# Two attention layers on one core: a fourth split step, outputs accumulated in DRAM, and projections in half blocks

## The chip, the cores and the metric

The kernel runs on one core of one Trainium2 chip. The core has a matrix engine (TensorE, PE in the profile, with its weight loads as PEld), a vector engine (VectorE, DVE), an activation engine (ScalarE, ACT), a general engine (GpSimd, POOL) and a queue engine (SyncE, SP) that here only issues transfers. Each engine executes its own instructions in order and waits for the others by semaphores. The metric is the device time of one execution in microseconds, the median of several runs.

## The reference, cut to what matters

The input x has 4 images of 64 x 64 tokens with 256 channels, so N = 4096 tokens each. Two attention layers follow one another, with no division by the root of the width:

```python
# layer 0: q, k are 32 wide, v is 256 wide
q, k, v = x @ Wq + bq, x @ Wk + bk, x @ Wv + bv
x = gamma * softmax(q @ k.T) @ v + x
# layer 1: f, g are 32 wide, v is 128 wide
f, g, v = x @ Wf + bf, x @ Wg + bg, x @ Wh + bh
x = x + (softmax(g @ f.T) @ v) @ Wo + bo
```

All values are float32. Layer 1 of an image needs layer 0 of the same image for all of its tokens, since every token is a key; different images are independent.

## The kernel before, in words

The work of an image is two stages, layer 0 and layer 1, and the images follow one another: one list of steps (b, l, j, i) is made at the end of `fast_path`, with b the image, l the layer, j the query block and i the step over keys. Layer 0 has 16 query blocks of 256 tokens with 8 steps of 512 keys. Layer 1 has 8 query blocks of 512 tokens with 16 steps of 256 keys.

A step's `scores` (L505) are products of keys and queries into one PSUM tile `st`, which has a single buffer; ScalarE takes the exponential of it (L517) into p. No maximum is subtracted. Scores are issued two steps ahead of the products that use them.

The products of p with the values need float32 accuracy, and there are two ways to get it. A *whole* step multiplies p and v as float32; each such product stands as two matmul instructions in the trace. A *split* step uses the faster fp32r type for parts. ScalarE makes a second exponential, with a slightly lowered exponent, rounded to fp32r: `high` (L515). VectorE subtracts it from p to get `low` (L522) and combines the two into `d` (L527). Three products (high with the values' part h, low with l, d with d) into two accumulators give the result (L536 in layer 0, L557 in layer 1). In layer 0 all steps are split. In layer 1 the steps 2, 7 and 12 of each block's 16 are, and the others are whole. In layer 1 VectorE also adds up p over the steps into `p_sum` (L698; at the first step a copy, L696), from which the softmax's denominators come; in layer 0 a column of ones in the values gives them.

Between the steps' own instructions lie *units*. `project_units` makes three or four for a block of 512 tokens: `transpose_unit` (squares of 32 x 32, which transfers have put in place, are transposed on VectorE, L381, and x is cut into two fp32r parts, L387 and L388), `qk_unit` (four products of 512 columns, L412; evictions L422 to L425; the result goes to DRAM, L428, and comes back as keys and queries by transfers from POOL, L472), and `v_unit` (products L442, evictions). The transposed x, the parts for two channel halves and the loaded squares lie in tiles `xT` (one buffer) and `squares` (five buffers of one channel half). `end_first` normalizes a layer-0 block and adds the residual (L585): the new x goes to DRAM for layer 1's projections (`x1_dram`, L590), and the same plus the output bias, added on POOL (L593), goes to a second DRAM tensor (`x1_res`, L594). `end_second` multiplies a layer-1 block by Wo (L624), gets denominators (L625 and L627), and adds the loaded `x1_res` rows to the scaled output on VectorE (L628); SP then writes `out` (L630). `load_old` (L605) loads those rows four steps ahead of a block's end.

The units of a block are spread evenly over its steps: `pace` and `upto` hand out so many at each step. Layer 1's projection of block (j-3)/2 is done in layer 0's block j for odd j from 3 on. Block 7 can't be done there, because its tokens come from the end of layer 0: it is done in layer 1's first block, whose last two steps (14 and 15) need its keys and values. The next image's layer-0 projections are done one block per query block of layer 1. Image 0's own first three blocks are projected before its first step, the other five in its first five steps.

The order of the instructions on an engine is laid down when the program is built. It follows the order of the text as a priority, but lets through what is expected to be ready sooner, so the trace can show another order than the text.

Of the kernel before, what the change touches and what calls it, by code (L numbers as in the profile page):

```python
# [60 lines left out]
S = 32  # L61
DOWN = 2.0**-13
EPS = 2.0**-12
AHEAD = 3

# [168 lines left out]
def fast_path(ctx: ExitStack, tc: tile.TileContext, x, w0, w1, wo, bo, gamma, out, off):  # L234
# [13 lines left out]
    split = [[l == 0 or i % 5 == 2 for i in range(NI[l])] for l in range(2)]  # L248
# [18 lines left out]
    def load_squares(key, tokens):  # L267

        turned[key] = []
        for c in range(NCC):  # L270
            t = work.tile([P, QB], F32, tag="squares", bufs=5, name=f"squares_{key[0]}_{key[1]}_{key[2]}_{c}")
            for a in range(P // S):
                ch = c * P + a * S
                nc.sync.dma_start(
                    t[a * S : (a + 1) * S, :].rearrange("j (b i) -> j b i", i=S),
                    tokens[:, ch : ch + S].rearrange("(b j) i -> j b i", j=S),
                )
            turned[key].append(t)

    def load_block(b, j):  # L280
        if b < B and j < NB:
            load_squares((b, 0, j), x[b, j * QB : (j + 1) * QB, :])


    x_nat = {}

    def load_first(j):
        if j < NB:
            x_nat[j] = []
            for n in range(j * NT, (j + 1) * NT):  # L290
                x_nat[j].append(data.tile([P, C], F32, tag="v1", bufs=V1, name=f"x_nat_{n}"))
                nc.sync.dma_start(x_nat[j][-1], x[0, n * P : (n + 1) * P, :])

    load_first(0)
    load_first(1)
# [8 lines left out]
    seen_v = const.tile([P, 2, B * NB, 2], F32, name="seen_v")  # L304
# [61 lines left out]
    xT, x_parts, k_t, v_t = {}, {}, {}, {}  # L366
    qk_dram, x1_dram, x1_res = {}, {}, {}
    q_t = {}


    def transpose_unit(b, l, j):
        def issue():
            xT[b, l, j] = data.tile([P, NCC, QB], F32, tag="xT", name=f"xT_{b}_{l}_{j}")
            for c in range(NCC):
                if b == l == 0:
                    ps = side_psum(f"psx_{j}_{c}")
                    for t in range(NT):
                        nc.tensor.transpose(ps[:, t * P : (t + 1) * P], x_nat[j][t][:, c * P : (c + 1) * P], ident)
                    nc.scalar.copy(xT[b, l, j][:, c, :], ps)
                else:  # L380
                    nc.vector.transpose(xT[b, l, j][:, c, :], turned[b, l, j][c])  # L381
            x_parts[b, l, j] = []
            for c in range(NCC):
                parts = [
                    work.tile([P, QB], F32R, tag="squares", bufs=5, name=f"x{what}_{b}_{l}_{j}_{c}") for what in "hl"
                ]
                nc.scalar.copy(parts[0], xT[b, l, j][:, c, :])  # L387
                nc.vector.tensor_sub(parts[1], xT[b, l, j][:, c, :], parts[0].bitcast(F32))  # L388
                x_parts[b, l, j].append(parts)
            if b == l == 0:  # L390
                load_first(j + 2)
            elif l == 0:
                load_block(b, j + 1)
            elif j == NB - 1:
                load_block(b + 1, 0)
# [3 lines left out]
    def split_values(v, h, low, d, seen):  # L399
        nc.scalar.activation(h, v, AF.Copy, scale=1.0 - DOWN)  # L400
        nc.scalar.activation(low, v, AF.Abs, accum_out=seen)
        nc.vector.scalar_tensor_tensor(d, h.bitcast(F32), -1.0 - EPS, v, ALU.mult, ALU.add)
        nc.vector.scalar_tensor_tensor(low, d.bitcast(F32), 1.0 / EPS, h.bitcast(F32), ALU.mult, ALU.add)
# [393 lines left out]
```

## Time and profile before

| | us |
|---|---|
| median of 3 runs | 3222.8 (3222.76 to 3225.62) |
| the profiled execution | 3222.18 |
| its span, first to last instruction | 3220.4 |
| PE busy | 3166.5 (98%) |
| DVE busy | 2691.5 (84%) |
| ACT busy | 1988.8 (62%) |
| POOL busy | 661.3 (21%) |

A row of the groups names the line, the engine, the operation, output and inputs with their shapes, the count, then the busy time, the mean duration in ns, and after a bar the time that the engine was idle just before them and what ended it. A row of the windows has a stretch in us from the span's start, its length, the busy time of PE, PEld, DVE, ACT and POOL with instruction counts, the granted share of the TensorE clock, and the transfers' share and rate. A line in order of time has start, duration, engine, line, operation, tiles and count, and in brackets the idle time before it with what ended it. SPq is the issuing of a transfer on SP.

### The profile page before, as it was taken

Reading aid. Unit: us, or ns where it says so; the run is one execution under the profiler, and the core shown is the slowest. Engines: PE = TensorE matmul, PEld = TensorE weight load, DVE = VectorE, ACT = ScalarE, POOL = GpSimd, SP = SyncE. Lnnn points to the kernel's source line nnn. Section 1 sums busy time; section 2 is a strip of 40 time slices with the busy share of each in tenths; the row PEclk is TensorE's granted clock in tenths of the full one; section 3 lists DMA queues with packets and bytes.
Section 4 is the critical chain, followed back from the end, with each engine's and each line's share of the span. In section 5 each row is a group of like instructions: output and inputs, shape, how many; then the busy total and the mean of one; then the engine's idle time right before and its main releaser. Section 6 shows DMA issues by size and latency. Waiting matters only on the chain. (4 is left out here: it accounts for less than half of the span.)

```text
span 3220.4 us, 51144 instructions
## 1 busy us (share of the span) xinstructions
PE 3166.5 (98%) x19460; PEld 2613.0 (81%) x19460; DVE 2691.5 (84%) x3181; ACT 1988.8 (62%) x2483; POOL 661.3 (21%) x784
## 2 busy tenths in 40 slices
PE   8999999999999999999999999999999999999998
PEld 7999997566799999655679999966558999995554
DVE  7888888888888888788888888878888888887776
ACT  6666666655566666565556666655555666665554
POOL 3222223000232222200022222310002222241000
PEclk9999999999999999999999999999999999999999
DMA  4111123221212112322121112232222211121110
GB/s 120 47 47 44 50 50 83 56 53 49 59 44 54 44 52 49 79 53 53 49 64 42 49 50 50 61 70 52 51 52 57 53 41 47 46 70 47 36 36 31
DMA packets 368653, 172.16 MB, mean 53 GB/s; under 512 B 257392, under 2 KB 343664, under 8 KB 368400
## 3 DMA queue, kind: packets, MB, share of 16 engines
q1 hardware_dynamic: 342528, 134.29, 16.0%
q0 software_dynamic: 24960, 34.18, 4.5%
q8 instruction: 157, 2.57, 0.3%
q14 instruction: 96, 0.79, 0.1%
q10 hardware_dynamic: 912, 0.33, 0.0%
HBM read 99.22 MB, written 67.11 MB: 52 GB/s over the span
## 5 line engine op out<-in xcount | busy, mean ns | idle before, releaser
L517 ACT ACTIVATE p<-st 128x1024 f32<-128x1024 f32 x1024 | 1044.5, 1020 | 393.6 <-PE st L505 369.5
L515 ACT ACTIVATE high<-st,down 128x1024 fp32r<-128x1024 f32 x608 | 678.8, 1116 | 683.6 <-PE st L505 572.7
L527 DVE SCALAR_TENSOR_TENSOR d<-low,high 128x1024 fp32r<-128x1024 f32 x608 | 761.2, 1252 | 208.3 <-PE acc L536 202.9
L522 DVE TENSOR_TENSOR low<-p,high 128x1024 fp32r<-128x1024 f32 x608 | 810.6, 1333 | 134.2 <-ACT p L517 134.2
L557 PE MATMUL acc<-p,v 128*128 128x512 f32 x1664 | 795.2, 597 | 0.0
L505 PE MATMUL st<-q,k 128*128 128x256 f32 (+1 forms) x3072 | 778.6, 361 | 8.4 <-ACT p L517 8.3
L698 DVE TENSOR_TENSOR p_sum<-p_sum,p 128x1024 f32<-128x1024 f32 x480 | 587.1, 1223 | 60.7 <-ACT p L517 47.5
L505 PEld LDWEIGHTS st<-q,k 128*128 128x128 f32 x3072 | 461.2, 189 | 210.7 <-ACT p L517 113.3
L536 PE MATMUL acc<-v0d,d 128*128 128x258 f32 x4096 | 591.7, 284 | 1.7 <-DVE d L527 1.6
L536 PE MATMUL acc<-v0h,high 128*128 128x258 f32 x4096 | 588.6, 283 | 1.6 <-ACT high L515 1.6
L536 PE MATMUL acc<-v0l,low 128*128 128x258 f32 x4096 | 587.0, 283 | 0.5 <-DVE low L522 0.5
L536 PEld LDWEIGHTS acc<-v0d,d 128*128 128x128 f32 x4096 | 533.1, 189 | 6.7 <-DVE d L527 3.6
L536 PEld LDWEIGHTS acc<-v0h,high 128*128 128x128 f32 x4096 | 534.1, 190 | 3.4 <-ACT high L515 2.0
L536 PEld LDWEIGHTS acc<-v0l,low 128*128 128x128 f32 x4096 | 532.7, 189 | 0.8 <-DVE low L522 0.7
L557 PEld LDWEIGHTS acc<-p,v 128*128 128x128 f32 x1664 | 308.4, 190 | 214.3 <-issue 184.7
L593 POOL TENSOR_TENSOR x_res<-x,bo 128x256 f32<-128x256 f32 x128 | 216.3, 1690 | 889.9 <-DVE g L583 482.0
L472 POOL DMA_DIRECT2D q<-qk_dram x252 | 123.9, 501 | 1166.1 <-PE st L505 1143.0
L676 POOL TENSOR_TENSOR x_res<-x_res,bv 128x256 f32<-128x256 f32 x128 | 189.6, 1482 | 114.4 <-DMA x_res<-in_x 85.0
L442 PE MATMUL psv<-wv,xT 128*128 128x128 f32 (+1 forms) x1024 | 194.8, 331 | 6.8 <-DVE qk L423 6.1
L442 PEld LDWEIGHTS psv<-wv,xT 128*128 128x128 f32 x1024 | 159.6, 192 | 29.8 <-DVE qk L423 8.5
L472 POOL DMA_DIRECT2D k<-qk_dram x224 | 109.6, 500 | 245.2 <-PE st L505 140.3
L388 DVE TENSOR_TENSOR xl<-xT,xh 128x512 fp32r<-128x512 f32 x128 | 87.1, 683 | 5.1 <-ACT xh L387 4.7
(96 smaller groups left out, 1701.9 us busy)
## 6 DMA issues: line engine op xcount, KB each, us to landing
x_res<-in_x SPq DMA_DIRECT2D x128, 128.0 KB, 2.2
qk_dram<-qk_parts SPq DMA_DIRECT2D x64, 256.0 KB, 2.1
x_dram<-x SPq DMA_DIRECT2D x128, 128.0 KB, 1.7
x_res<-x_res SPq DMA_DIRECT2D x128, 128.0 KB, 1.7
squares<-x_dram SPq DMA_DIRECT2D x256, 64.0 KB, 2.3
x_old<-x_res SPq DMA_DIRECT2D x128, 128.0 KB, 2.0
out<-x_old SPq DMA_DIRECT2D x128, 128.0 KB, 1.7
q<-qk_dram POOLq DMA_DIRECT2D x252, 64.0 KB, 2.1
```

What stands on the lines that cost most here:

```text
L442: nc.tensor.matmul(ps[:, t, :], xT[key][:, c, (t0 + t) * P : (t0 + t + 1) * P], wv[l][:, c, :], start=(c == 0), stop=(c == NCC - 1),)
L472: nc.gpsimd.dma_start(dst[n * D : (n + 1) * D, :], parts[h, which])
L505: nc.tensor.matmul(st[:, g, :], k_t[b, l, kt // NT][:, kt % NT * P : (kt % NT + 1) * P], q_t[b, l, j * n // QB][:, q0 : q0 + n], start=Tru ...
L515: nc.scalar.activation(self.high, s_flat, AF.Exp, bias=down)
L517: nc.scalar.activation(self.p, s_flat, AF.Exp)
L522: nc.vector.tensor_sub(self.low, self.p, self.high.bitcast(F32))
L527: nc.vector.scalar_tensor_tensor(self.d, self.low.bitcast(F32), -1.0 / EPS, self.high.bitcast(F32), ALU.mult, ALU.add)
L536: nc.tensor.matmul(acc[2 * s + which][:, :W], p[:, g * QB0 + s * P : g * QB0 + (s + 1) * P], v0[self.i][v][:, g, :], start=self.first and ...
L557: nc.tensor.matmul(acc[which], v[:, g, :], p[:, g * QB : (g + 1) * QB], start=first and g == 0, stop=last and g == G[1] - 1,)
L593: nc.gpsimd.tensor_add(x_old[s], x_new[s], bo_sb)
L676: nc.gpsimd.tensor_add(x_res[b, j][t], x_res[b, j][t], bv)
L698: nc.vector.tensor_add(p_sum, p_sum, s.p)
```

## The change

In layer 1, four steps per block (`SPLIT1` = 2, 6, 10, 14) are split instead of three. Layer 0's residual with the bias goes to `out` directly; `x1_res` and `load_old` are gone. Layer 1's output is scaled on ScalarE and added to `out` in DRAM by an accumulating transfer from POOL. The sum of p begins with an addition at step 1. Projections are made for half blocks of 256 tokens, with the two channel halves in one instruction where that is possible; a unit's products have 256 columns. The loads of squares are issued half by half: behind the projection of the half before. At the start of image 0 two halves are under way, the odd ones in buffers of the split values. The even spreading is replaced by `plan`, which puts each unit at a step: in layer 0's block j the three units of half j-2 at steps 0, 4 and 5; in layer 1's first block halves 14 and 15 at steps 0, 2, 3 and 6, 8, 9; the next image's halves every seven steps from step 12 of the first block on; a finished block's end units at steps 1 and following of the next.

The diff, cut to its core; what stands at the places left out is the same renaming of blocks to halves, buffers and loads of image 0's start:

```diff
+SPLIT1 = (2, 6, 10, 14)
...
-    split = [[l == 0 or i % 5 == 2 for i in range(NI[l])] for l in range(2)]
+    NH = N // QB0
+    split = [[l == 0 or i in SPLIT1 for i in range(NI[l])] for l in range(2)]
...
     def load_squares(key, tokens):
-        turned[key] = []
+        t = work.tile([P, NCC, QB0], F32, tag="squares", bufs=2, name="squares_" + "_".join(map(str, key)))
         for c in range(NCC):
-            t = work.tile([P, QB], F32, tag="squares", bufs=5, name=f"squares_{key[0]}_{key[1]}_{key[2]}_{c}")
             for a in range(P // S):
                 ch = c * P + a * S
                 nc.sync.dma_start(
-                    t[a * S : (a + 1) * S, :].rearrange("j (b i) -> j b i", i=S),
+                    t[a * S : (a + 1) * S, c, :].rearrange("j (b i) -> j b i", i=S),
                     tokens[:, ch : ch + S].rearrange("(b j) i -> j b i", j=S),
                 )
-            turned[key].append(t)
+        turned[key] = t
...
+            lead = b == l == 0 and h % 2 == 1
+            tag = "v1_parts" if lead else "xT"
+            xT[key] = data.tile([P, NCC, QB0], F32, tag=tag, bufs=LEAD_BUFS if lead else 1, name=f"xT_{b}_{l}_{h}")
...
+                nc.vector.transpose(
+                    xT[key].rearrange("p c n -> p (c n)"), turned[key].rearrange("p c n -> p (c n)")
+                )
...
+            nc.scalar.copy(x_parts[key][0], xT[key])
+            nc.vector.tensor_sub(x_parts[key][1], xT[key], x_parts[key][0].bitcast(F32))
...
-            nc.sync.dma_start(qk_dram[key].rearrange("h w d n -> (h w d) n"), parts.bitcast(F32))
+            nc.sync.dma_start(qk_dram[b, l, j].rearrange("h w d n -> (h w d) n")[:, cols], parts.bitcast(F32))
+            halves[b, l, j] = part + 1
+            if l == 0 and b > 0:
+                load_half(b, h + 1)
+            elif l == 1 and h == NH - 1:
+                load_half(b + 1, 0)
+            elif l == 1:
+                load_squares((b, 1, h + 1), waiting.pop((b, h + 1)))
...
+        def add_up(self, p_sum):
+            if self.l == 0:
+                return
+            if self.i == 0:
+                first_p.append(self.p)
+            elif self.i == 1:
+                nc.vector.tensor_add(p_sum, first_p.pop(0), self.p)
+            else:
+                nc.vector.tensor_add(p_sum, p_sum, self.p)
...
-                if part == QB // QB0 - 1 and s == NS - 1:
-                    load_squares((b, 1, jj), x1_dram[b, jj])
+                if s == NS - 1:
+                    tokens = x1_dram[b, jj][part * QB0 : (part + 1) * QB0, :]
+                    if j == 0:
+                        load_squares((b, 1, j), tokens)
+                    else:
+                        waiting[b, j] = tokens
                 nc.gpsimd.tensor_add(x_old[s], x_new[s], bo_sb)
-                nc.sync.dma_start(x1_res[b, jj][row : row + P, :], x_old[s])
+                nc.sync.dma_start(out[b, n * P - b * N : (n + 1) * P - b * N, :], x_old[s])
...
-                nc.vector.scalar_tensor_tensor(y[t], ps[:, :C], inverse[:, 1, n : n + 1], y[t], ALU.mult, ALU.add)
+                y = small(f"y_{key}_{t}")
+                nc.scalar.activation(y, ps[:, :C], AF.Copy, scale=inverse[:, 1, n : n + 1])
                 row = j * QB + t * P
-                nc.sync.dma_start(out[b, row : row + P, :], y[t])
+                nc.gpsimd.dma_start(out[b, row : row + P, :], y, accum_op=ALU.add)
...
+    def plan(b, l, j, ends):
+        units = {}
+        def put(i, *some):
+            units.setdefault(i, []).extend(some)
+        if l == 0:
+            if j >= 2:
+                t, qk, v = project_units(b, 1, j - 2)
+                put(0, t), put(4, qk), put(5, v)
+            for n, u in enumerate(ends):
+                put(1 + n, u)
+            return units
+        if j == 0:
+            for n, u in enumerate(ends):
+                put(1 + n, u)
+            for n, h in enumerate((NH - 2, NH - 1)):
+                t, qk, v = project_units(b, 1, h)
+                put(6 * n, t), put(6 * n + 2, qk), put(6 * n + 3, v)
+        else:
+            for n, u in enumerate(ends):
+                put(1 + n, u)
+        if b + 1 < B:
+            for h in range(NH):
+                i = 12 + 7 * h - j * NI[1]
+                for n, u in zip((0, 2, 3), project_units(b + 1, 0, h)):
+                    if 0 <= i + n < NI[1]:
+                        put(i + n, u)
+        return units
...
-        if l == 1 and s.i == NI[1] - 4:
-            load_old(b, j)
...
-        pace = NI[l] - (5 if l == 1 else 1)
-        upto = min(len(units), -(-len(units) * (s.i + 1) // pace))
-        todo = units[done:upto]
-        done = upto
+        s.add_up(p_sum)
+        todo = units.get(s.i, [])
```

## The prediction

> **What bounds the kernel now.** I read the page's first section, the groups of instructions, a table of windows by stage, and the order of time of single engines around the one place where the windows differ.
>
> ```profile
> PE 3166.5 (98%) x19460; PEld 2613.0 (81%) x19460; DVE 2691.5 (84%) x3181; ACT 1988.8 (62%) x2483; POOL 661.3 (21%) x784
> ...
> L628 DVE SCALAR_TENSOR_TENSOR x_old<-pso,inverse,x_old 128x256 f32<-128x256 f32 x128 | 61.5, 481 | 3.4 <-DVE inverse L627 0.3 <-DMA x_old<-x_res 0.3
> L696 DVE COPY p_sum<-p 128x1024 f32<-128x1024 f32 x32 | 23.8, 745 | 2.7 <-ACT p L517 0.2
> ...
> core 0: us, PE busy (x) PEld busy (x) DVE busy (x) ACT busy (x) POOL busy (x), PEclk, DMA share, GB/s
> 854.90:1306.80 451.90, 451.90 (x3718) 448.31 (x3717) 385.97 (x435) 293.59 (x356) 130.23 (x126) 1.00 0.20 51
> 1311.80:1363.90 52.10, 46.43 (x149) 26.37 (x147) 41.42 (x51) 28.95 (x43) 6.28 (x10) 0.97 0.33 71
> 1445.90:1487.70 41.80, 41.56 (x141) 25.01 (x139) 35.51 (x44) 24.62 (x31) 1.96 (x4) 1.00 0.20 51
> 2902.60:2947.00 44.40, 40.12 (x128) 21.84 (x126) 33.76 (x39) 23.61 (x32) 7.41 (x10) 1.00 0.22 56
> 3020.00:3057.20 37.20, 36.89 (x121) 21.27 (x119) 29.30 (x34) 19.94 (x21) 1.96 (x4) 1.00 0.12 36
> ```
>
> The rows are the first layer of image 1, the first and a later query block of its second layer, then the same two of image 3. TensorE is the bound almost everywhere, but its busy time hides small stalls, because matmul records overlap. I therefore use distances between starts. A row of twelve whole products takes 5.31 us including the last one's tail: 0.43 us each. Two 512-column products of parts span 0.62 us where one lasts 0.39: 0.23 us apart. Those of 258 columns are 0.12 apart, those of 256 too. So a plain second-layer step is 4 x 0.43 + 2 x 0.23 = 2.18 us of TensorE, a split one 8 x 0.233 = 1.86. Priced so, all matmuls sum to about 3125 us. The first layer (451.9 us) lies on this floor. A later second-layer block is 0.8 us above it with projections in it (41.8 against 41.0) and 0.6 without. The *first* block of each second layer is 8.1, 9.7, 9.7 and 6.4 us above it: 33.9 us together. The first query block of all lies 9.3 us above (57.1 against 47.8), and 8 us at the end hold no compute.
>
> Why the first block stalls, in image 1 (start, duration, engine):
>
> ```profile
> 1319.36 4.11 SPq L274 DMA_DIRECT2D squares<-x_dram  x8
> 1327.57 0.70 DVE L381 STREAM_TRANSPOSE xT<-squares 128x512 f32<-128x512 f32 x1
> 1333.62 0.70 DVE L381 STREAM_TRANSPOSE xT<-squares 128x512 f32<-128x512 f32 x1
> 1340.45 0.34 SPq L428 DMA_DIRECT2D qk_dram<-qk_parts  x1
> 1342.98 1.98 POOL L472 DMA_DIRECT2D k<-qk_dram  x4 [24.53 <-DMA qk_dram<-qk_parts]
> 1353.44 1.99 PE L442 MATMUL psv<-wv,xT 128*128 128x256 f32 x8 [1.84 <-DVE qk L423]
> 1355.08 0.81 PE L505 MATMUL st<-q,k 128*128 128x512 f32 x2
> ```
>
> Block 7's tokens exist only when the first layer has ended. From there one chain runs: squares, two transposes, projection, DRAM, keys. The scores of step 14 need those keys; they land near 1346.6 (last issue 1344.5 plus 2.1), and scores that would be due near 1340 start at 1355.1. The squares were in by 1325.3, but VectorE's second transpose stood behind other work until 1333.6; and the next image's projections stood ahead of the scores in TensorE's order and waited for VectorE themselves. In image 3, without them, the scores start as the keys land (2938.7).
>
> **What the Trainium skill says.** "TensorE: Matmul & The Clock Gate", part 1, says that an idle array falls to half clock for a window of about 3.4 us. The trace agrees: the granted clock is 0.50 from 1345.0 to 1348.4 and again from 2140.3 to 2143.7, both in these first blocks, so such a stall costs about 1.7 us more. "DMA: Bandwidth & Descriptors", SWDGE vs HWDGE vs iDMA, says that accumulating transfers come from GpSimd alone; its rules for kernel authors add that an accumulate must wait for the earlier write of the same bytes. No run here shows an accumulate yet. Here the earlier write lies a layer back. "ScalarE: Activation LUTs", What happens when an `exp` ACTIVATE runs, gives about 0.09 us for each pointer operand; the trace agrees (1116 ns with a bias tile, 1020 without).
>
> **The change part by part.** The sum is made on the profiled execution (span 3220.4, its own time 3222.2); the median 3222.8 is 0.6 higher, which I ignore.
>
> 1. *A fourth split step in each of 32 second-layer blocks.* Four whole products at 0.43 (1.72 us) become six at 0.233 (1.40): 0.32 less. 32 x 0.32 = **-10 us**. ScalarE gets 32 exponentials of 1.12 (36 us), VectorE 32 x 2.44 (78 us), where its low and d take 1.22 each in this layer.
>
> 2. *First block of the second layer.* Half 14 is now done at steps 0 to 3. Half 15's residual moves from step 0 to 2, yet in the trace it was already written only at 1316.7, where step 2 starts. Its squares queue on SP behind the x1 and out writes and half 14's qk write, so I put them at 1320.5, plus 4.1 of issues and 2.3 of landing: 1327. The transpose is one instruction now, planned at step 6 (1326), qk at step 8 (1330), four steps later than before. In image 3 the way from the end of that projection to the scores took 10.1 us (2928.6 to 2938.7); with half-width evictions I take 9. So keys land near 1340.5, scores of 14 are due at 1339.8, and no other projection stands in the way before step 14, as the next image begins at step 12. Step 14 is split now and wants low and d soon after. I take 3 us left in each image: 12 instead of 33.9, **-22 us**. Bounds: nothing left (-34), or all of it left (0).
>
> 3. *Later blocks.* A split step's chain from its scores: exponentials 0.2+2.0, low 1.2, d 1.2, and up to one addition of p_sum between (1.1): 4.6 to 5.7 us. TensorE has 5.3 us of work meanwhile, so it waits up to 0.4 us, unless an output or a projection falls into those two steps. Today this shows once in an image-3 block (0.45 us at step 12). Of the new steps 2 and 6 are covered by outputs at steps 1 to 4; 10 and 14 often aren't. 28 later blocks x 0.2 = **+5 us**. Bounds: -8 (VectorE is relieved) to +15.
>
> 4. *Outputs.* Removed: 128 VectorE operations of 481 ns, 128 loads and 128 residual writes; the residual write now goes to out, so SP issues 256 fewer. Added: 128 ScalarE scalings and 128 accumulates on POOL. A scaling is bounded by 0.39 (the 128x258 copy out of PSUM) and 0.48 (plus the skill's pointer); I take 0.48, 61 us. An accumulate's issue is bounded by 0.50 (32 rows) and 0.86 (128 rows of wqk_whole); I take 0.86, 110 us on an engine 21% busy. Queued behind a waiting accumulate on POOL are the next block's q and, in the last block, the next image's keys; POOL now waits 35 to 40 us for scores before each q, so that hides it; uncovered it would cost the scores directly. Hidden in the middle. At the end the last accumulate lands 1.7 (a plain write) to 3.7 us (a read first) after issue: **+1 us** (0 to 3).
>
> 5. *Sum of p.* 32 copies of 745 ns go, and the addition starts at step 1; VectorE -24 us, hidden. The first p is held a step longer; the third step's p is in another tag, so a buffer is there.
>
> 6. *Half blocks.* TensorE: a block's four 512-column projections (4 x 0.233) become eight of 256 (8 x 0.118): 64 x 0.012 = **+1 us**. VectorE's qk pair (740 and 694 ns) has some 0.37 us of fixed part beyond 512 elements at 0.96 per ns, paid twice: +24 us; ScalarE likewise +23. SP: 448 loads of squares become 896 of half size, at 0.51 us of issue: +229 us, and 64 more qk writes; POOL 32 more short key issues in the first image. SP's queue has no other user that is short of time, because a half's squares are asked for five steps (12 us) before their transpose and need 6.4. With two buffers a load waits until the previous half's projection has read its parts; it is issued just behind that projection, so this wait is short. If that cover is gone, the transpose is late and everything behind it on VectorE.
>
> 7. *Start.* The first block of image 0 lies 9.3 us above the floor, with ScalarE and VectorE nearly full. Two halves in flight in separate buffers overlap more, the extra fixed parts take some back: **-3 us** (-7 to +4).
>
> Engine totals after: VectorE -61-24+78+24+3 (values of the new split) = +20 on 2691; ScalarE 36+61+23 = +120 on 1989. Neither becomes the bound on average.
>
> Sum: -10 -22 +5 +1 +1 -3 = -28: 3222.8 - 28 = **3195 us**.
>
> **The rivals.**
>
> *The wait stays.* Half 15 is projected at step 8 instead of 4, and the order on an engine isn't that of the text: the second transpose came 8 us after its data. If that recurs, 8.5 us stay per image: 3195 + 4 x 5.5 = 3217. For it: the chain is as long as the four steps left. Against it: one transpose instead of two, no second projection in the way.
>
> *More goes than I count.* The first blocks lose all (-12), the start 3 more and the later blocks 8: 3172. For it: more distance at every transpose. Against it: the uncovered splits.
>
> *Late d, slower.* There are 128 split steps. VectorE runs in order, and if one more addition of p_sum (1.13 us between starts) stands ahead of each d, TensorE waits that much: 128 x 1.13 = +145, 3340. It decides from 28/128 = 0.22 us per split step on. For it: four steps need 4 x 1.13 + 2 x 1.13 = 6.8 us of VectorE in 8.4, before projections; and scores have one buffer, which a split step holds 2.8 us (scores 0.46, exponentials 2.0, gaps 0.3) against a step of 1.86, and a plain one 1.83 against 2.18, so that three plain steps only just win it back. Against it: VectorE is 15% free over a block (35.5 of 41.8 now); 2.7 us are taken off per block (part 4 and 5) for 2.4 added.
>
> **How the numbers follow.** The likeliest (3181 to 3210) has 0.60, more goes 0.17, the wait stays 0.13, late d 0.10. Changes within 0.2% (6.4 us) can hardly be told from none. Faster: 0.60 + 0.17 + half of the second rival (3217 lies at the border 3216.4) = 0.83; same 0.07; slower 0.10. Range: from 3172 (middle of "more goes") to 3214; outside lie half of that, most of "the wait stays" and "late d", about 2 in 10.
>
> **What would show it.** Right: 52.1 and 44.4 us for the first blocks fall to about 42 (with one half of the next image in it) and 39; no half-clock window before the end; later blocks near 42, and 37 in image 3; 128 split steps; accumulates on POOL with no one waiting. Wrong: the keys of half 15 still awaited several us (part 2), d awaited over 0.22 us in each split step (part 3), PE waiting for psv or qk evictions (part 6), or an end longer by several us (part 4).

## The result: nothing that can be told from no change

The changed kernel takes 3221.3 us (median of 12 runs, 3218.98 to 3227.74) against 3223.7 (12 runs, 3222.34 to 3225.62): a ratio of 0.9995, 95% interval 0.9987 to 1.0003. The prediction was 3195 us, faster, with a range of 3172 to 3214. Medians here and below are of fast executions alone; the only two slow ones, 3760 and 8098 us, are of the experiment "half 15 early" and left out. The profiled execution spans 3217.8 us where the one before spanned 3220.4.

The first section of the page of the changed kernel (busy time, share of the span, instructions):

```profile
PE 3161.6 (98%) x19780; PEld 2635.8 (82%) x19780; DVE 2690.5 (84%) x3221; ACT 2084.5 (65%) x2771; POOL 763.5 (24%) x948
```

VectorE's output operation and its copy of p are gone from the groups; for the outputs these two stand there now (count, then busy time and mean ns of one, then idle time before them and what ended it):

```profile
L655 POOL DMA_DIRECT2D out<-y x128 | 112.3, 884 | 510.1 <-ACT y L653 504.5 <-issue 5.2
L653 ACT ACTIVATE y<-pso,inverse 128x256 f32<-128x256 f32 x128 | 60.6, 473 | 11.9 <-DVE inverse L650 11.5
```

And the same five windows as in the prediction, moved to where the stages lie now (stretch in us; its length; busy time of each engine; granted clock; DMA share; GB/s):

```profile
859.80:1310.50 450.70, 450.06 (x3747) 449.25 (x3747) 381.72 (x445) 296.47 (x375) 121.58 (x126) 1.00 0.21 51
1310.50:1354.00 43.50, 40.41 (x143) 23.45 (x141) 36.36 (x43) 26.66 (x40) 6.29 (x10) 1.00 0.24 52
1436.80:1479.20 42.40, 42.37 (x151) 26.25 (x150) 36.35 (x45) 28.32 (x41) 5.53 (x8) 1.00 0.25 41
2888.30:2930.90 42.60, 38.34 (x131) 21.43 (x129) 33.89 (x40) 24.38 (x34) 6.30 (x10) 1.00 0.15 38
3006.80:3044.80 38.00, 37.28 (x123) 21.46 (x121) 28.97 (x31) 22.43 (x26) 5.54 (x8) 1.00 0.15 21
```

The first block of image 1's second layer fell from 52.1 to 43.5 us, of which 3.8 are matmuls that now lie elsewhere and 4.8 time above the floor; that of image 3 from 44.4 to 42.6. A later block of image 3 rose from 37.2 to 38.0, although it has 0.3 us less matmul. VectorE and ScalarE have no more work than predicted (VectorE 2690.5 us against 2711, ScalarE 2084.5 against 2109), so the miss is in waits.

To see where, I split each span into the matmuls priced as in the prediction (the floor) and the time above it in five stretches. They add up to the span (us; "later" are the later blocks of all second layers, the last one included, "end" from the last product of all on). Another count, with prices a little different and blocks cut elsewhere, moves single entries by up to 2 us:

| | floor | to the end of image 0's first layer | other first layers | first blocks | later | end | span |
|---|---|---|---|---|---|---|---|
| before | 3125.4 | 25.6 | 1.3 | 34.0 | 22.0 | 12.1 | 3220.4 |
| predicted | 3116 | 23 | 1 | 12 | 27 | 13 | 3192 |
| changed | 3116.0 | 28.0 | 1.6 | 21.0 | 33.1 | 18.2 | 3217.8 |

The floor is right. The first blocks miss by 9, the later ones by 6, the end by 5, the start by 5: 25 us, all of what failed to come.

**The later blocks.** VectorE and TensorE around the split step at 10 of a block of image 3 in the changed kernel (start, duration, engine, what the idle time before waited for):

```profile
3067.78 1.23 DVE L543 TENSOR_TENSOR low<-p,high 128x1024 fp32r<-128x1024 f32 x1 [1.88 <-ACT p L539]
3068.93 1.22 DVE L560 TENSOR_TENSOR p_sum<-p_sum,p 128x1024 f32<-128x1024 f32 x1
3070.06 1.22 DVE L548 SCALAR_TENSOR_TENSOR d<-low,high 128x1024 fp32r<-128x1024 f32 x1
3071.33 0.73 PE L585 MATMUL acc<-d,v 128*128 128x512 f32 x2 [0.34 <-DVE d L548]
```

VectorE has been idle for 1.88 us, makes low, and then adds this step's p to p_sum (1.1 us) *before* it makes d, for which TensorE waits. The same happens at step 14. The kernel before has the same order, and there one such wait shows per block of image 3, at step 12:

```profile
3048.09 1.22 DVE L698 TENSOR_TENSOR p_sum<-p_sum,p 128x1024 f32<-128x1024 f32 x1
3050.49 0.73 PE L557 MATMUL acc<-d,v 128*128 128x512 f32 x2 [0.31 <-DVE d L527]
```

**The first blocks.** TensorE at the end of image 3's first block, and GpSimd's load of the late keys:

```profile
2916.72 1.99 POOL L490 DMA_DIRECT2D k<-qk_dram  x4 [23.26 <-DMA qk_dram<-qk_parts]
...
2916.83 5.31 PE L585 MATMUL acc<-p,v 128*128 128x512 f32 x12
2921.58 1.03 PE L527 MATMUL st<-q,k 128*128 128x512 f32 x2
2923.86 0.73 PE L585 MATMUL acc<-high,v 128*128 128x512 f32 x2 [1.25 <-ACT high L537]
2924.78 0.73 PE L527 MATMUL st<-q,k 128*128 128x512 f32 x2 [0.18 <-ACT p L539]
2926.04 0.73 PE L585 MATMUL acc<-low,v 128*128 128x512 f32 x2 [0.53 <-DVE low L543]
2926.68 0.73 PE L527 MATMUL st<-q,k 128*128 128x512 f32 x2
2928.52 0.50 PE L527 MATMUL st<-q,k 128*128 128x512 f32 x1 [1.11 <-ACT p L539]
```

TensorE has used up all its other products when step 14's scores can start; and step 14 is split, so high, p and low are each awaited behind late scores: 3.1 us in four waits.

### The profile page after: what moved, and what is told of

It reads as the page before. It is cut to its first block, busy times and chain, and to the rows that moved or that the text cites. A ratio compares the mean times of both kernels' runs of the same rounds, so it can differ in the third digit from the quotient of the medians.

```text
span 3217.8 us, 53549 instructions
## 1 busy us (share of the span) xinstructions
PE 3161.6 (98%) x19780; PEld 2635.8 (82%) x19780; DVE 2690.5 (84%) x3221; ACT 2084.5 (65%) x2771; POOL 763.5 (24%) x948
## 5 line engine op out<-in xcount | busy, mean ns | idle before, releaser
L537 ACT ACTIVATE high<-st,down 128x1024 fp32r<-128x1024 f32 x640 | 714.7, 1117 | 695.9 <-PE st L527 551.4
L543 DVE TENSOR_TENSOR low<-p,high 128x1024 fp32r<-128x1024 f32 x640 | 859.1, 1342 | 162.3 <-ACT p L539 162.1
L548 DVE SCALAR_TENSOR_TENSOR d<-low,high 128x1024 fp32r<-128x1024 f32 x640 | 789.0, 1233 | 228.3 <-PE acc L567 225.6
L527 PE MATMUL st<-q,k 128*128 128x256 f32 (+1 forms) x3072 | 761.4, 355 | 7.0 <-ACT p L539 5.4
L585 PE MATMUL acc<-p,v 128*128 128x512 f32 x1536 | 726.9, 596 | 0.0
L560 DVE TENSOR_TENSOR p_sum<-p_sum,p 128x1024 f32<-128x1024 f32 x448 | 547.5, 1222 | 15.5 <-ACT p L539 3.2
L585 PEld LDWEIGHTS acc<-p,v 128*128 128x128 f32 x1536 | 282.5, 189 | 207.5 <-issue 185.0
L624 POOL TENSOR_TENSOR x_res<-x,bo 128x256 f32<-128x256 f32 x128 | 200.9, 1569 | 885.9 <-DVE x L613 885.8
L655 POOL DMA_DIRECT2D out<-y x128 | 112.3, 884 | 510.1 <-ACT y L653 504.5
L730 POOL TENSOR_TENSOR x_res<-x_res,bv 128x256 f32<-128x256 f32 x128 | 175.2, 1369 | 70.3 <-DMA x_res<-in_x 69.9
```

Of the source, the lines that this page charges most:

```text
L527: nc.tensor.matmul(st[:, g, :], k_t[b, l, kt // NT][:, kt % NT * P : (kt % NT + 1) * P], q_t[b, l, j * n // QB][:, q0 : q0 + n], start=Tru ...
L537: nc.scalar.activation(self.high, s_flat, AF.Exp, bias=down)
L543: nc.vector.tensor_sub(self.low, self.p, self.high.bitcast(F32))
L548: nc.vector.scalar_tensor_tensor(self.d, self.low.bitcast(F32), -UP, self.high.bitcast(F32), ALU.mult, ALU.add)
L560: nc.vector.tensor_add(p_sum, p_sum, self.p)
L585: nc.tensor.matmul(acc[which], v_part[:, g, :], p[:, g * QB : (g + 1) * QB], start=first and g == 0, stop=last and g == G[1] - 1,)
```

## The experiments

Times are medians, with the ratio to the kernel before where it carries the argument; the us by stretch are those of the table above, from the one profiled execution of each kernel. Medians may be compared across experiments: the kernel before took 3222.8 to 3223.7 us beside each. Some expectations count the later blocks 2 us lower than the table does (23.7 us where the table has 25.7).

**Is it the addition ahead of d?** The "late addition", in the changed kernel:

```diff
-            if self.i == 0:
+            if self.i == 0 or self.split:
                 first_p.append(self.p)
...
                 nc.vector.tensor_add(p_sum, p_sum, self.p)
+                while first_p:
+                    nc.vector.tensor_add(p_sum, p_sum, first_p.pop(0))
```

> The changed kernel with one thing moved: in the second layers the p of a split step is added to p_sum only after the next step's addition, so that VectorE goes straight from low to d at every split step; the same additions are made, one step later. Theory A (what costs in the later blocks is that d stands behind the split step's own addition of 1.1 us): the waits of the d products at steps 10 and 14 of image 3's blocks (0.34 to 0.5 us each) go, a block of image 3 falls from 37.97 us to 37.0 to 37.3, the other images' sixteen-step blocks lose about 1 us per image, the first blocks perhaps 1 us each; the whole is 8 to 12 us shorter, 3209 to 3213. Rival (the single buffer of scores, which ScalarE must have read twice at a split step, sets the pace, and VectorE's order is not the limit): a block of image 3 stays within 0.2 us of 37.97 and the whole within 3 us.

Measured: 3204.4 us, 0.9940 (0.9927 to 0.9954), more than expected. First blocks 21.0 to 12.2 us, later 33.1 to 25.7, an image-3 block 37.97 to 37.25. VectorE and TensorE at the same step:

```profile
3057.97 1.23 DVE L543 TENSOR_TENSOR low<-p,high 128x1024 fp32r<-128x1024 f32 x1 [1.62 <-ACT p L539]
3059.30 1.23 DVE L548 SCALAR_TENSOR_TENSOR d<-low,high 128x1024 fp32r<-128x1024 f32 x1
3060.44 1.22 DVE L560 TENSOR_TENSOR p_sum<-p_sum,p 128x1024 f32<-128x1024 f32 x1
3061.08 0.62 PE L587 MATMUL acc<-d,v 128*128 128x512 f32 x2
```

d follows low, and its product waits for nothing. The rival, scores' single buffer, would have left the block at 37.97.

**Was the addition a cost before, too?** The kernel before with the late addition alone:

> The kernel before (three split steps, block-wide projections) with the late addition of a split step's p alone. Theory A says that the addition between low and d costs there too, where no output covers the split step: one wait of 0.45 us per block in image 3 goes, an image-3 block falls from 37.17 to about 36.8, other later blocks by 0.1 to 0.3, and the first blocks' 33.9 us excess, which comes from the projections' order, falls by at most 4: 4 to 10 us shorter, 3213 to 3219. Rival (the cost of the addition only exists with four split steps): no change, 3221 to 3225.

Measured: 3208.2 us, 0.9953 (0.9937 to 0.9970): 15 us, more than expected. Its later blocks fall from 22.0 to 9.0 us above the floor, an image-3 block to 36.68, the first blocks only from 34.0 to 31.3. So part of the old kernel's time above the floor was this order as well; I had seen it once (0.45 us at step 12) and not asked what stood ahead of d.

**What is the fourth split step worth?** `SPLIT1 = (2, 7, 12)` in the changed kernel, then with the late addition, then with half 15 early (the next experiment) as well. The first of these has the addition ahead of d, as the changed kernel has; where its expectation says that d comes straight after low, it is mistaken.

> The changed kernel with three split steps in each second layer again, at 2, 7 and 12 of 16, and everything else as changed (accumulating outputs, half blocks, d straight after low in the order). It undoes part 1 alone. If part 1 gave its 10 us of matmuls and part 3's loss belongs to the fourth step (one more uncovered d), the matmul floor rises by 10 us, a block of image 3 comes out at 37.2 to 37.5 us (0.43 us per block dearer in matmuls, about 0.9 us less waiting), and the whole is 0 to 4 us longer than the changed kernel. If the fourth step loses nothing, 8 to 11 us longer. If it loses more than it gives, shorter.

> The changed kernel with three split steps (2, 7, 12) and the late addition. With the addition in between, three split steps were 11 us shorter than four. If that was the addition alone, four steps are now the better: this one is 5 to 10 us longer than four steps with the late addition (3204.4), 3209 to 3214, with image-3 blocks of 37.0 us or more. If a split step costs something else besides (scores' single buffer, ScalarE's second exponential), three stay better or equal: 3198 to 3204, with image-3 blocks at 36.7 to 37.2.

> The kernel with the late addition and half 15 early (3193.6 us with four split steps), but with three split steps, at 2, 7 and 12. It isolates part 1 where nothing else disturbs it. The floor rises by 10.1 us. In the pair without half 15 early the later blocks' excess was 23.7 us with four and 18.8 with three; if that carries over and the first blocks stay near 0.7 us, three steps are 5 us longer: 3197 to 3200. If the first blocks now lose 1 us each with three, 3201 to 3203; if the fourth step is worth nothing, 3193.

Measured, three against four split steps: 3209.9 against 3221.3 in the changed kernel, 3202.7 against 3204.4 with the late addition (too close to tell apart: 3197.7 to 3203.7 and 3202.8 to 3207.6), 3197.9 against 3193.6 with both. In the changed kernel the fourth step loses 11 us, the case that I had named last and without a size: the floor gives 10.2, but first blocks (11.4 with three, 21.0 with four) and later ones (23.7, 33.1) take 19. With both mended it is a gain of 4 us, as expected: 10.2 from the floor, less 5.9 in the later blocks (25.9 with four, 20.0 with three), with first blocks near nothing in either. Part of the changed kernel's first-block loss came from having a split step, 14, right behind the late keys. With 12 the last one, step 14 is whole: the keys are issued as late as with four (27.9 and 28.0 us after the block's first product in image 1), but step 14 then loses nothing where it lost 2.9 us.

**Is half 15 too late by plan?** "Half 15 early", in the changed kernel and then with the late addition:

```diff
-                put(6 * n, t), put(6 * n + 2, qk), put(6 * n + 3, v)
+                put(5 * n, t), put(4 * n + 2, qk), put(5 * n + 3, v)
```

> The changed kernel with the units of half block 15 in the first block of each second layer one step or two earlier: transpose at step 5, projection at 6, values at 8, instead of 6, 8 and 9. Theory A (the chain from half 15's squares to the keys is late because the plan puts its units late and its copies stand behind the exponentials of the split step): the keys of the last quarter come 2 to 3 us earlier, the first blocks' excess over the matmuls falls from 4.9, 4.9, 4.9, 6.2 us by 2 to 4 each, the whole 6 to 12 us shorter, 3209 to 3215. Rival (the squares of half 15 land too late, since SyncE holds the last of them behind the wait of half 14's write, and the transpose then makes VectorE wait and delays the split step's parts): no gain, or up to 1 us per block lost.

> The changed kernel with the late addition of a split step's p and half 15's units at steps 5, 6 and 8. The first alone took the first blocks' excess from 20.9 to 12.2 us, the second alone to 17.4. If the two act on different waits they add: first blocks 8 to 9 us together, the whole near 3201. If the late addition already lets half 15's chain through early enough that only the landing of its squares is left, the second adds nothing or costs 1 us per image: 3204 to 3208.

Measured: 3217.5 us (0.9982, 0.9974 to 0.9990) alone; first blocks 17.5, short of what I expected. With the late addition 3193.6 (0.9910, 0.9893 to 0.9926), more than expected; first blocks 0.7 for all four images together. I call this kernel, with both edits, the mended one. The two edits give 17 and 4 alone and 28 together. In image 1, counted from the block's first product, half 15's squares have landed by 13.1 us in all four kernels. Its transpose starts at 16.9 in the changed kernel, 15.7 with half 15 early, 13.5 with the late addition and 13.5 with both, so the late addition takes it out of VectorE's queue. But only with both is the projection also early enough (from 14.9 us, against 17.7 or later) for its evictions to come before the exponentials of split step 6, and the keys are issued at 21.4 us instead of 26.9 to 28.0. The same stretch of image 3 then:

```profile
2892.99 1.98 POOL L490 DMA_DIRECT2D k<-qk_dram  x4 [16.65 <-DMA qk_dram<-qk_parts]
...
2903.47 1.02 PE L587 MATMUL acc<-high,v 128*128 128x512 f32 x2
2904.34 0.73 PE L527 MATMUL st<-q,k 128*128 128x512 f32 x2
2904.91 0.63 PE L587 MATMUL acc<-low,v 128*128 128x512 f32 x2
2905.39 0.62 PE L587 MATMUL acc<-d,v 128*128 128x512 f32 x2
```

From keys to step 14's products are 10.5 us instead of 7.1, and nothing waits. The rival (squares landing too late) falls: VectorE never idles for them in these kernels. With both edits the transpose follows their landing by 0.4 us, so little more can be had there.

**What do the accumulating outputs cost?** The last block's outputs alone written plainly (old rows read from out, VectorE's operation, SyncE's write), then all outputs, then all outputs in the mended kernel. The core of the edit:

```diff
+            x_old[b, j].append(small(f"x1_old_{b}_{j}_{t}"))
+            nc.sync.dma_start(x_old[b, j][t], out[b, j * QB + t * P : j * QB + (t + 1) * P, :])
...
+                if (b, j) in x_old:
+                    y = x_old[b, j][t]
+                    nc.vector.scalar_tensor_tensor(y, ps[:, :C], inverse[:, 1, n : n + 1], y, ALU.mult, ALU.add)
+                    nc.sync.dma_start(out[b, row : row + P, :], y)
+                    return
```

> The changed kernel, except that the last block of the last image reads its old rows of out at step 12, scales and adds on VectorE and writes them plainly from SyncE, as the kernel before did; all other second-layer outputs still accumulate. Theory A (the 6 us that the end grew by come from the last four accumulating transfers: a landing of 3.1 us instead of 1.7, and a drain of GpSimd's queue that takes 6.7 us instead of 3.2): from the last product's end to the span's end 14.9 to 15.5 us instead of 21.05, the whole 5 to 6 us shorter. Rival B (the longer drain is paid once when a kernel has used accumulating transfers at all): only the landing comes back, 1.5 to 2.5 us. Nothing else should move by more than 1 us.

> The changed kernel with part 4 undone: every second-layer output reads its old rows of out at step 12, scales and adds on VectorE and is written plainly from SyncE; no transfer accumulates. The run with only the last block so kept a drain of 6.35 us on GpSimd at the end, so the longer drain isn't tied to the last transfers. Theory (it is paid once if any transfer has accumulated): with none, the drain falls to 3.2 us and the time from the last product's end to the span's end from 21.0 to 15 us. Rival (GpSimd's drain is longer for another reason, more issues of any kind): it stays near 6.4 and the end near 19.6. Elsewhere VectorE gets 128 operations of 0.48 us back and ScalarE loses 128 of 0.47: the blocks of image 3 stay at 37.97 us if the addition ahead of d is what they wait for. Whole: 5 to 7 us shorter than changed by the theory, 1 to 2 by the rival.

> The kernel with the late addition and half 15 early (3193.6 us), with part 4 undone: old rows of out read at step 12, scaled and added on VectorE, written from SyncE. In the changed kernel that took the end from 21.0 to 18.7 us after the last product and left the blocks of image 3 at 37.9. If outputs are hidden in the middle either way, 2 to 3 us shorter: 3190 to 3192. If VectorE's 128 operations of 0.48 us more matter now that d follows low directly, the later blocks lose 0.1 to 0.3 us each, 28 of them: 3193 to 3199.

Measured: 3222.5 us (0.9994, 0.9986 to 1.0003), 3219.6 (0.9987, 0.9980 to 0.9994) and 3193.8 against 3193.6. The end falls from 18.2 to 16.8 us in the first and 15.8 in the second; blocks of image 3 stay at 37.97 and 37.9. So the later blocks hide the outputs either way, and the accumulates cost 2.4 us at the end. In the mended kernel plain outputs gave nothing: the end fell by 1.8 us, but a first block lay about 1.2 us above its floor instead of 0.6, 2.5 us in all. My theory of the drain (the instruction DRAIN, which stands at the end of GpSimd's program) fell: with not one accumulate left, it still takes 6.1 us. The first run's gain was drowned: first blocks at 26.7, for a reason given at the end.

**What makes the drain, and the late start?** In the kernel before with the late addition, image 0's key loads cut in halves; and in the mended kernel the same loads issued by SyncE:

```diff
-                load_k(b, l, j, near)
+                load_k(b, l, j, near, 2)
```

```diff
-            nc.gpsimd.dma_start(dst[n * D : (n + 1) * D, :], parts[h, which])
+            if engine:
+                engine.dma_start(dst[n * D : (n + 1) * D, :].bitcast(F32), parts[h, which].bitcast(F32))
+            else:
+                nc.gpsimd.dma_start(dst[n * D : (n + 1) * D, :], parts[h, which])
...
+        engine = None if parts is None else nc.sync
```

> The kernel before with the late addition (3208.2 us by itself), and in image 0 each load of keys and of the first queries issued from GpSimd in two halves of 256 columns: 36 more issues, 548 instead of 512, as the changed kernel has, and still no accumulating transfer. Two things are asked. (1) GpSimd's drain at the end: the changed kernel with no accumulating transfer left still drained for 6.11 us against 3.17 before. If the number of issues from GpSimd or their half width in image 0 makes it, this run drains for about 6 us; if it is anything else in the changed kernel, 3.2 us. (2) The first query block of image 0 ended at 97.4 us before and at 98.5 to 102.6 us in the changed kernel's relatives: if GpSimd's doubled issues of keys make it late, it ends 1 to 3 us later here, if the half-width evictions do, at 97.4 as before.

> The changed kernel with the late addition and half 15 early (3193.6 us), and image 0's keys, which GpSimd copies from SBUF in halves, issued from SyncE instead: 64 issues fewer on GpSimd (612 instead of 676, accumulates included). Drain: if the number of issues makes it long, it stays at 6.3 to 6.7 us; if the half-width copies at the start do, it falls to 3.2. Start: if GpSimd's eight issues of 0.5 us per block hold the first keys back, image 0's first query block ends 1 to 3 us sooner than 98.5; if SyncE's queue, which also issues the first image's rows and the writes of keys, is no freer, it stays or gets up to 2 us later. Whole: 3189 to 3195.

Measured: 3212.0 us against 3208.2, and 3188.8 (0.9892, 0.9876 to 0.9909) against 3193.6. GpSimd's drain at the end of the changed kernel (times: shortest, median and longest of three, in ns; start of the first and last):

```profile
L829 POOLq DRAIN  x3: 50/107/6679, 3210.2 to 3217.5; - x3
```

In the kernel before:

```profile
L784 POOLq DRAIN  x3: 50/107/3167, 3216.4 to 3220.1; - x3
```

In the changed kernel with no accumulating output:

```profile
L846 POOLq DRAIN  x3: 50/107/6107, 3210.9 to 3217.6; - x3
```

In the kernel before with the late addition and its first keys cut in halves:

```profile
L790 POOLq DRAIN  x3: 50/107/6107, 3202.2 to 3208.8; - x3
```

In the mended kernel with the first keys from SyncE:

```profile
L835 POOLq DRAIN  x3: 50/107/1452, 3186.9 to 3188.9; - x3
```

GpSimd issues 68, 36, 68, 72 and 4 copies from SBUF to SBUF in these five. The drain goes with these copies, all made in the first 90 us, and not with the number of issues (612 in the last of the five, 512 in the kernel before). The start: cutting the loads made the way to the end of image 0's first layer 1.6 us longer (25.5 to 27.1), which would be 1.6 of the 2.4 us that the changed kernel lost there. That is one execution each, and the start scatters: in eight profiled executions of the changed kernel and its relatives with the same order of instructions there, image 0's second layer began between 519.4 and 521.9 us, against 518.4 and 518.5 in the two with the start of the kernel before. So the start did get slower, by 1 to 3.5 us. The medians bear out the cut loads' part (3.8 us longer in all, 2.5 of them at the end). SyncE as issuer shows no gain at the start (26.4 to 30.0, with a stretch of half clock from 19.3 to 22.7 us in the second): that part of the expectation failed. The whole fell by 4.8 us, where the drain alone is 5.2 us shorter.

**What is left in the later blocks?** An output's matmuls can cover a wait, that is, give TensorE other work meanwhile. The outputs at other steps, in the fastest kernel twice and then in the changed kernel, all else untouched (shown with the second one's steps):

```diff
         else:
-            for n, u in enumerate(ends):
-                put(1 + n, u)
+            for n, u in zip((2, 6, 10, 14), ends):
+                put(n, u)
```

> The fastest kernel so far (late addition, half 15 early, image 0's keys from SyncE; 3188.8 us) with the four outputs of the block before at steps 0, 4, 8 and 12 of a later block instead of 1 to 4, so that none falls into a split step. With outputs at 1 to 4 an image-3 block still lies 0.97 us above its matmuls, where the kernel before with the late addition, which spread them, lies 0.10 above. If ScalarE's scaling of an output between the two exponentials and the next scores is what delays the split step at 2, the blocks of image 3 fall from 37.24 to 36.4 to 36.7, the later blocks' 23.7 us by 8 to 15, the whole to 3174 to 3181. If outputs' covering of split steps matters more, blocks lengthen: 3190 or more.

> The same kernel with the outputs at the split steps themselves, 2, 6, 10 and 14: each puts 0.6 us of TensorE work between the scores and the split products. If cover for a late d is what a split step lacks, the later blocks' 23.7 us fall by 8 or more (image-3 blocks at 36.4 to 36.8) and this is the better of the two: 3174 to 3181. If ScalarE's turn is what is short there, the scaling makes it worse: image-3 blocks at 37.5 or more, 3192 or more.

> The changed kernel itself, with the split step's own addition still ahead of d, and the outputs at steps 2, 6, 10 and 14. The prediction priced part 3 by cover: a split step with an output in it doesn't wait for d, one without waits up to 0.4 us. If that is so, the waits for d at steps 10 and 14 go, an image-3 block falls from 37.97 to 36.9 to 37.3, and the whole is 8 to 15 us shorter, 3206 to 3213. If cover doesn't help while the addition stands ahead of d, no change within 3 us.

Measured: 3177.6 us with steps 0, 4, 8, 12 (0.9857, 0.9840 to 0.9873), 3180.0 with 2, 6, 10, 14 (0.9865, 0.9848 to 0.9881; in its range, but not the better of the two), and, more than expected, 3202.0 for the changed kernel with nothing but outputs at its split steps (0.9939, 0.9922 to 0.9955). There the addition still stands ahead of d, but the output's matmuls lie before the products (same step of image 3):

```profile
3055.43 1.22 DVE L560 TENSOR_TENSOR p_sum<-p_sum,p 128x1024 f32<-128x1024 f32 x1
3055.87 0.59 PE L647 MATMUL pso<-wo,o 128*128 128x256 f32 x2
3056.57 1.22 DVE L548 SCALAR_TENSOR_TENSOR d<-low,high 128x1024 fp32r<-128x1024 f32 x1
3056.86 0.28 PE L648 MATMUL pso<-ones,sums 128*128 128x1 f32 x2
3057.55 0.61 PE L585 MATMUL acc<-low,v 128*128 128x512 f32 x2
3058.00 0.62 PE L585 MATMUL acc<-d,v 128*128 128x512 f32 x2
```

Later blocks fall from 33.1 to 14.5 us; an image-3 block from 37.97 to 36.5. The move also thins out steps 1 to 4, but in image 3 the gain lies where cover was missing: steps 10 and 14 lay 0.65 us each above the floor and now lie 0.07. Cover alone mends them, and with it the late addition adds nothing there (14.5 here, 16.7 in the fastest kernel with its outputs at the same steps). It leaves the first blocks (23.6), which have no such outputs. Whether ScalarE's turn matters too stays open: with outputs between the split steps image 3's blocks stay at 37.2, with 36.4 to 36.7 expected, while the other images' blocks gain more than with outputs at the split steps (about 1.8 us more per image).

The version with late addition, half 15 early, SyncE's first keys and outputs at 0, 4, 8, 12 is 44 us faster than the changed kernel and 45 faster than the one before.

## Why the prediction was wrong

**Part 1, right.** The floor fell by 9.4 us, with part 6's +1 as predicted.

**Part 2 failed in its residue: "I take 3 us left in each image".** 5.2 us stayed on average. The chain came within 2 us of the forecast up to the keys in image 1: transpose 1327.8 (1326), projection 1331.2 (1330), keys near 1342.6 (1340.5). That was partly luck. The squares landed at 1323.9, 3 us sooner than the 1327 forecast, and the transpose then stood 3.9 us behind other work of VectorE: the rival "the wait stays" at half its 8 us. The 3 us had no working behind them. Step 14, which I named as split and wanting low and d soon, lost 2.9 us alone behind its late keys, and the waits for d at steps 2 and 6 of the same block (0.89 and 0.31 us in image 1) were left out. With d straight after low the first blocks fall to 12.2. That this is the 12 predicted is a coincidence; with half 15 early as well they fall to 0.7.

**Part 3 failed in its size: "28 later blocks x 0.2 = +5 us".** It was +11.1. The mechanism was named exactly, up to one addition between low and d, up to 0.4 us, steps 10 and 14 uncovered. What was mis-sized is the price, 0.4 us per block on average instead of 0.2, and it wasn't spread over 28 blocks. In image 3, which has no next image's projections as cover, both uncovered steps wait, about 0.5 us each by the distance of starts (0.34 and 0.36 as the trace puts it). A block there rose by 0.8 us with 0.3 us less matmul: 1.1 for each of seven, some 8 of the 11 us. The other 21 blocks lost about 0.15 each, less than forecast.

So one order on VectorE cost most of both: the late addition gives back 8.8 us in the first blocks and 7.4 in the later ones, 16.2 where the two parts had missed by 15. This was my rival "late d" with the price 0.13 us per split step (16.2/128, the late transpose in the first blocks included) instead of 1.13: below the 0.22 us from which I had it decide, and enough, with the end and the start, to take the gain.

**Part 4, right in kind.** The accumulates cost 2.4 us at the end (+1, bounds 0 to 3) and nothing in the changed kernel's later blocks; an accumulate took 3.1 us from issue to landing, and the scaling 473 ns, inside its bounds of 0.39 and 0.48. (The price of a pointer operand in the upper bound stands in another section of the Trainium skill's "ScalarE: Activation LUTs" than the prediction names: What ACT_TABLE_LOAD costs.)

**Part 6 failed where it costs nothing: "POOL 32 more short key issues in the first image".** They took about 1.6 us at the start and 2.9 of drain at the end. With the accumulates' 2.4 that leaves 0.8 of the end's 6.1 us unexplained. The halves' fixed part on VectorE was as forecast: an eviction pair of qk took 742 and 685 ns in one piece and 472 and 419 ns per half, 0.36 us more per block. No run undoes the half blocks alone; the first layers, 1.6 us above the floor against 1.3, show no loss from them.

**Part 7 failed in sign.** The start lost 2.4 us in the profiled executions (1 to 3.5 with the scatter) instead of gaining 3; about 1.6 is the key copies', the rest I didn't settle.

**Part 5** was undone by no run alone, so that it is hidden isn't shown. The half-clock windows of the first blocks went from this execution, as forecast, but not from every relative's (below).

## What to carry to other kernels

When a product of parts, as in a split step, needs a chain of VectorE operations, look at what else stands in that engine's order between the links: an addition that nobody waits for can be issued after the link that TensorE waits for. Put small independent matmuls, such as outputs, where the chain is exposed rather than all at the start of a block. And don't put the most latency-bound step right behind the last data to arrive.

## What the runs showed that I had not expected

- GpSimd's drain at a kernel's end took 1.5, 3.2 and 6.1 us with 4, 36 and 68 to 72 copies from SBUF to SBUF issued by it in the first 90 us, with 3100 us between. Why isn't shown, nor whether the type of the copies matters: those from SyncE were also declared float32 on both sides. Accumulates added 0.6 at most.
- The same stall at the end of a first block sometimes brings a half-clock window and sometimes doesn't. In the kernel with one block of plain outputs scores waited 1.17 us there in image 1, and so they did in the changed kernel. Its granted clock was 0.50 from 1353.0 to 1356.4; this row starts 0.4 us late and so shows 0.56:

```profile
1353.40:1356.80 3.40, 3.40 (x7) 1.54 (x5) 2.26 (x4) 1.02 (x1) 0.00 (x0) 0.56 0.13 40
```

  In the changed kernel it stayed at 1.00:

```profile
1351.60:1354.00 2.40, 2.39 (x9) 1.45 (x9) 2.37 (x4) 1.26 (x2) 0.00 (x0) 1.00 0.32 83
```

  The Trainium skill ("TensorE: Matmul & The Clock Gate", part 1) gives such a window about 3.4 us, which agrees. Such windows came in three of that kernel's four first blocks, which together were 5.7 us longer than the changed kernel's (26.7 against 21.0); that hid the gain at its end. Image 3's first block has one such window with the late addition and two in the changed kernel with outputs at its split steps and in the kernel before with the late addition, so their first-block figures hold some of it.
